# Splitting some steps' exponentials between ScalarE and VectorE, and reordering the last parts, in a two-layer conv-attention kernel

## The chip, the cores and the metric

The kernel runs on one core of a Trainium2 chip. The metric is device time in microseconds (us) of that core. A core has five engines that run their own instruction queues in order: TensorE (PE: matmuls), VectorE (DVE), ScalarE (ACT: exponentials and other functions), GpSimd (POOL) and SyncE (SP, which here issues nearly all DMAs). They wait for each other through semaphores. Matmul results go to PSUM, everything else lives in SBUF or in device memory.

## What is computed

The input is `x`, 4 images of 64x64 pixels with 128 channels, all fp32. The reference, cut to what matters here:

```
# layer 0, per image (N = 4096 pixels)
c2 = conv3x3(conv3x3(elu(x), W1), W2);  a, b = split(c2);  c3 = a * sigmoid(b)
q, k, v = c3 @ Wq, c3 @ Wk, c3 @ Wv                     # 4, 4 and 16 columns
x = x + c3 + (softmax(strictly causal q k^T / 4) @ v, tiled 8 times) @ W3
# layer 1, per image
t = layernorm(x)                                        # 4096 tokens
q, k, v = t @ wq, t @ wk, t @ wv                        # 16 heads of 8
h = t + (softmax(q k^T) @ v) @ wo                       # all 4096 x 4096 pairs, 16 heads
t = x + h + (silu(h @ w1) * (h @ w3)) @ w2              # hidden 344
y = layernorm(t);  out = t + mixture of 8 experts, the best 2 of them by a router
```

By far the most work is in the attention of layer 1: 4 images x 16 heads x 4096 x 4096 exponentials, that is 1.07e9 of them, or 8.4e6 for each of the 128 lanes of an engine.

## The kernel before

All of it is in `fast_path` (line 116). (A second function, `general_path`, is a fallback for inputs with large scores and isn't run with these inputs.) Every engine is used through `InOrder` (line 95), which keeps an engine's instructions in the order in which the Python code emits them. So the order of the emission is the order of each queue.

**The attention step** (`attention_step`, line 772) is the unit of the main loop. A segment is a group `g` of four heads, a chunk `c` of 512 queries and a range of key tiles; a step is one tile of 128 keys `kt` of a segment. There are 4 images x 4 groups x 8 chunks x 32 key tiles = 4096 steps. A step has two halves:

- `scores()` takes two PSUM tiles of 128x1024 from `s_tile` (pool `f_ps_s`, line 134, which holds three such tiles in turn), fills each with two matmuls (`s<-qx,f_kx`, one per head), and lets ScalarE take the exponential of each into an SBUF tile `e` (pool `f_ep`, 8 tiles).
- `values()` multiplies the four heads' exponentials with the values (`acc<-e,vg`, four heads) and adds up in one PSUM bank `acc` over the key tiles of the segment. At the segment's last tile VectorE copies `acc` to `at`, and SP writes it to memory (`d_a<-at`).

**The turn.** The main loop (lines 1190 to 1214) makes one step a turn: `do_step` emits the step's scores and exponentials and puts its `values` on the list `undone`; `finish(2)` at the end of the turn emits the values of the step before the last two. So TensorE works two steps behind ScalarE with the values. The steps of layer 0's attention (`first_step`, 144 of them) go through the same loop when they are there.

**Fillers.** All other work is cut into pieces by Python generators and put between the steps: `first_attention` (line 528, the convolutions, layer 0's attention and the operands of layer 1 of the next image) and `last_part` (line 815, one per chunk: output projection, feed-forward, router, experts). A generator yields after each piece of TensorE work of about 0.46 us; "held" means that the same PSUM bank is filled further, "stop" that an operation of another engine follows. `insert()` (line 239) emits one piece. A turn emits at most one piece, when `credit` is above zero; `credit` grows each turn by a rate such that the fillers (planned at `PREPARE` = 149.0 us an image and `LAST` = 20.8 us a chunk, line 1179) come out spread over the remaining steps, and is capped at 0.7. Pieces use the single PSUM bank `m` (`m_tile`). Some yields carry no TensorE work (0.0): they are turns in which a chain waits for a DMA or another engine. `last_part` has eight of them at its start (its operands are loaded; the reciprocal of the sums goes to memory and comes back broadcast as `per`) and six before the small product with the experts' biases (`eb`), whose operand `g8` goes to memory and back.

After the last step the loop ends, and `run_alone` emits what is left of the fillers: with at least the last chunk's whole `last_part`, since its attention has only just ended.

Of the kernel before, what the change touches and what calls it, by code (L numbers as in the profile page):

```python
# [92 lines left out]


class InOrder:


    def __init__(self, tc, engine):
        self._tc, self._engine, self._last = tc, engine, None

    def __getattr__(self, name):
        op = getattr(self._engine, name)

        def call(*args, **kw):
            made = op(*args, **kw)  # L105
            if self._last is not None:
                after = mybir.DependencyInfo(mybir.DependencyClass.NoSync, mybir.DependencyReason.DATA)
                self._tc.add_manual_dep(made.ins, self._last, after, reason="as written")
            self._last = made.ins.name
            return made  # L110

        return call
# [3 lines left out]
def fast_path(ctx: ExitStack, tc: tile.TileContext, a: dict, where: dict, out: bass.AP, verdict):  # L116
# [12 lines left out]
    big = ctx.enter_context(tc.tile_pool(name="f_big", bufs=1))  # L129
    ep = ctx.enter_context(tc.tile_pool(name="f_ep", bufs=8))  # L130
    wk = ctx.enter_context(tc.tile_pool(name="f_wk", bufs=2))
# [18 lines left out]
    def chunk(tag, name=None):  # L150
        return wk.tile([P, QB], FP, tag=tag, bufs=CHUNKS.get(tag, 1), name=name or tag)

    def small(name, dims):
# [67 lines left out]

    steps_in, undone, fillers = [], [], []

    def do_step(step):
        scores, values = step
        undone.append((values, scores()))

    def finish(leave):
        while len(undone) > leave:
            values, es = undone.pop(0)  # L230
            values(es)

    def advance(part):
# [70 lines left out]
    def spread(eng, taps, u_all):  # L304
# [23 lines left out]
        spread_of.append(u_all)  # L328

    def row_terms(band):  # L330
        r = wk.tile([P, 4, 8, IMG + 2], FP, tag="r", bufs=1, name="r")
        for i, (x, y, op) in enumerate(SUMS):
            pool.tensor_tensor(r[:, i], band[:, x : x + 15 : 2, :], band[:, y : y + 15 : 2, :], op)
        return r
# [267 lines left out]
    def second_operands(b, st):  # L602
# [58 lines left out]
        for k in range(4):  # L661
            product(by_g[:, k], yT[:, k * P : (k + 1) * P], wv1)
            if k == 1:
                yield 0.46, "held"
        vc = wk.tile([P, 4 * NH1, 1 + HD1], FP, tag="vc", bufs=1, name="vc")
        pool.memset(vc[:, :, 0:1], 1.0)
# [30 lines left out]
    def first_step(c, r, qx0, sums, found):  # L697
# [49 lines left out]

        return scores, values

# [21 lines left out]

    def attention_step(b, seg, kt, place, qx, vg, part):
        g, c = seg.g, seg.c

        def scores():
            ss, es = [s_tile(), s_tile()], []
            for j in range(NSLOT):
                r = slice(j * SLOT, (j + 1) * SLOT)
                pe.matmul(
                    ss[j // 2][:, (j % 2) * QB : (j % 2 + 1) * QB],  # L780
                    lhsT=kx[r, place * P : (place + 1) * P].bitcast(FR),
                    rhs=qx[r, :].bitcast(FR),
                    start=True,
                    stop=True,
                )
            for s in ss:
                e = e_tile()
                act.activation(e, s, AF.Exp)
                es.append(e)
            return es  # L790

        def values(es):
            for j in range(NSLOT):
                pe.matmul(
                    acc[j * SLOT : j * SLOT + 1 + HD1, :],
                    lhsT=vg[:, kt // 4, kt % 4, j, :],
                    rhs=es[j // 2][:, (j % 2) * QB : (j % 2 + 1) * QB],
                    start=kt == seg.lo,
                    stop=kt == seg.hi - 1,
                )  # L800
            if kt == seg.hi - 1:
                at = chunk("at1")
                if part:
                    dve.tensor_tensor(at, acc, part[0], ALU.add)
                else:
                    dve.tensor_copy(at, acc)
                to = scratch[b]["a"][c, g] if seg.hi == NT else scratch[b]["p"][g, c]
                sp.dma_start(out=to, in_=at)
                if seg.hi == NT and g == NG1 - 1:
                    fillers.append([last_part(b, c), LAST])  # L810

        return scores, values


    def last_part(b, c):
        d = scratch[b]
# [8 lines left out]
        for _ in range(3):  # L825
            yield 0.0, "stop"
        dve.reciprocal(rs, rs)
# [4 lines left out]
        )  # L832
        for _ in range(4):
            yield 0.0, "stop"
        dve.tensor_tensor(an, an, per, ALU.mult)
        yield 0.0, "stop"
        ps = bank()
# [100 lines left out]
        for b_ in range(4):  # L938
            sp.dma_start(out=g8.rearrange("e (k b a) -> b e k a", k=4, a=SLOT)[b_], in_=by_block[b_, :NE])
        for _ in range(6):  # L940
            yield 0.0, "stop"

        ps = bank()
        tokens(ps, g8, eb, range(2))
        yield 0.46, "held"
        tokens(ps, g8, eb, range(2, 4))
        dve.tensor_tensor(t, ps, t, ALU.add)
        yield 0.46, "stop"
        for k in range(4):
            tk = t[:, k * C : (k + 1) * C]  # L950
            by_e = wk.tile([P, NE, C], FP, tag="two", bufs=1, name="by_e")
            for half in range(2):
# [8 lines left out]
                if half == 1:  # L961
                    added = chunk("w", "added")[:, :C]
                    dve.tensor_reduce(added, by_e.rearrange("p e c -> p c e"), AX.X, ALU.add)
                    dve.tensor_tensor(tk, tk, added, ALU.add)
                yield 0.46, "stop"
        sp.dma_start(out=tb_o[b][:, 4 * c : 4 * c + 4, :], in_=by_k(t))

# [151 lines left out]
    steps_left = [sum(s.hi - s.lo for s in plan if s.b == b) for b in range(B)]  # L1119
    now, quiet = [0], [False]  # L1120

    def stream():
# [16 lines left out]
        for at, seg in enumerate(plan):  # L1139
# [13 lines left out]
            for kt in range(seg.lo, seg.hi):  # L1153
# [3 lines left out]
                if seg.lo > 0 and kt == seg.lo + 4:  # L1157

                    part.append(chunk("part"))
                    sp.dma_start(out=part[0], in_=scratch[seg.b]["p"][seg.g, seg.c])  # L1160
                yield attention_step(seg.b, seg, kt, 8 * seg.place(kt // 8) + kt % 8, qx, vg, part)
                if follower and follower not in ahead and follower.ready():
# [15 lines left out]

    PREPARE, LAST = 149.0, 20.8
    st = batches[0]  # L1180
# [4 lines left out]

    fillers.extend([gen, PREPARE] for gen in reversed(left[1:]) if gen is not st.conv)

    steps = stream()
    credit, waiting = 0.0, False
    while True:  # L1190
        if steps_in:
            do_step(steps_in.pop(0))
        else:
# [4 lines left out]
            if waiting:  # L1198
                finish(0)
            else:  # L1200
                do_step(step)
        b = now[0]
        if batches[b].second == NQ and len(batches) == b + 1 and b + 1 < B:
            Batch(b + 1)
            fillers.append([first_attention(b + 1, batches[b + 1]), PREPARE])

        rate = 1.0
        if batches[b].second == NQ:
            within = steps_left[b] - 40 if b + 1 < B else min(steps_left[b] - 40, 160)
            rate = sum(us for _, us in fillers) / max(1, within)  # L1210
        credit = min(0.7, credit + rate)
        if waiting or credit > 0.0 and not quiet[0]:
            credit -= insert()
        finish(2)
    finish(0)
    alone[0] = True
# [718 lines left out]
```

## Time and profile before

| what | value |
|---|---|
| time of the runs, median of 3 | 8253.63 us (8251.3 to 8255.63) |
| the profiled execution: its time | 8256.29 us |
| the profiled execution: first to last instruction (span) | 8254.1 us |
| mean granted TensorE clock | 0.985 |
| busy: PE | 8010.7 us (97%) |
| busy: ACT | 7886.0 us (96%) |
| busy: DVE | 2513.9 us (30%) |
| busy: POOL | 712.2 us (9%) |
| instructions: DVE / ACT | 5118 / 8699 |
| main loop, roughly | 220 us to 8171 us of the span |

All times below are of the one profiled execution unless it is said otherwise; its own time is 8256.29 us, 2.66 us above the median of the runs. An entry of the timeline gives the start in us from the span's start, the length in us, the engine, the line, the operation, the tiles written and read, and how many equal ones were merged. Since every engine is used through `InOrder`, all instructions carry the line of that helper (L105), so that one goes by the names of tiles. "Busy" of TensorE is the union of the matmuls' intervals; matmuls overlap, so it is no measure of how near to its limit TensorE is. Likewise an exponential's interval (about 1.1 us) is longer than the distance between the ends of two that follow each other.

### The profile page before, as it was taken

How to read it: one execution, taken by the hardware profiler on the slowest of the kernel's cores; microseconds unless marked ns; L12 is line 12 of the kernel's file. 1: busy time of each engine (PE TensorE's matmuls, PEld its weight loads, DVE VectorE, ACT ScalarE, POOL GpSimd, SP SyncE). 2: the span in 40 equal slices, each digit the busy share in tenths (PEclk: the TensorE clock that was granted, in tenths of full speed). 3: DMA queues.
4: the chain of work that ended last, by engine and by line, in shares of the span. 5: the costliest groups of instructions: out<-in, count | busy, mean ns of one | idle time of the engine just before them, and what ended most of it. 6: DMA issues, size and time to landing. Idle time of an engine off the chain costs nothing.

```text
span 8254.1 us, 172356 instructions
## 1 busy us (share of the span) xinstructions
PE 8010.7 (97%) x72957; PEld 2492.4 (30%) x72957; DVE 2513.9 (30%) x5118; ACT 7886.0 (96%) x8699; POOL 712.2 (9%) x631
## 2 busy tenths in 40 slices
PE   4899999999999999999999999999999999999997
PEld 3222222223332322333333333233333333332233
DVE  7433222222322223333322222343332222221223
ACT  1799999999999999999999999999999999999996
POOL 5101211000000003110000000311100000000000
PEclk8899999999999999999999999999999999999998
DMA  1222010101100001111100000111111111111211
GB/s 51 76 69 68 24 41 31 55 29 50 42 24 28 26 19 35 36 39 45 39 31 24 27 28 19 33 36 48 35 42 49 47 38 46 52 37 38 66 61 37
DMA packets 213937, 334.19 MB, mean 40 GB/s; under 512 B 31555, under 2 KB 107811, under 8 KB 213155
## 3 DMA queue, kind: packets, MB, share of 16 engines
q1 hardware_dynamic: 209139, 321.31, 11.9%
q8 instruction: 574, 9.40, 0.5%
q10 hardware_dynamic: 4016, 1.77, 0.1%
q14 instruction: 208, 1.70, 0.1%
HBM read 195.09 MB, written 127.93 MB: 39 GB/s over the span
## 4 chain that ended last, share of the span: by engine, by line
PE 86%; issue 7%; DVE 3%; ACT 1%; DMA 1%; POOL 1%; SPq 0%; ACTq 0%; POOLq 0%; DVEq 0%
PE acc L105 41%; PE s L105 29%; PE m L105 16%; ACT e L105 1%; DVE h L105 1%; POOL v L105 0%; DVE t L105 0%; DMA xe<-in_x_dram 0%; DMA f_kx<-d_k 0%; SPq L105 0%; POOL rs L105 0%; DMA d_r<-sums 0%; DVE added L105 0%; DVE sums L105 0%; POOL xt L105 0%
## 5 line engine op out<-in xcount | busy, mean ns | idle before, releaser
L105 ACT ACTIVATE e<-s 128x1024 f32<-128x1024 f32 (+1 forms) x8480 | 7813.8, 1101 | 100.5 <-PE s L105 95.5
L105 PE MATMUL acc<-e,vg 128*9 128x512 f32 x32768 | 4337.4, 595 | 1.4 <-DVE at L105 1.4
L105 PE MATMUL s<-qx,f_kx 32*128 32x512 f32 (+2 forms) x16960 | 2918.2, 496 | 49.2 <-ACT e L105 33.5
L105 PEld LDWEIGHTS s<-qx,f_kx 32*128 32x128 f32 (+1 forms) x16960 | 1168.8, 182 | 4105.3 <-ACT e L105 3882.9
L105 PEld LDWEIGHTS acc<-e,vg 128*9 128x9 f32 x32768 | 717.0, 90 | 797.2 <-issue 462.1
L105 PE MATMUL m<-v,f_wino 128*32 128x256 f32 x5328 | 432.2, 397 | 5.4 <-DVE t L105 3.5
L105 DVE TENSOR_TENSOR by_e<-m,gates 128x512 f32<-128x512 f32 x245 | 169.5, 692 | 682.0 <-PE m L105 682.0
L105 POOL TENSOR_TENSOR v<-r 128x1024 f32<-128x1024 f32 x128 | 248.7, 1949 | 1172.8 <-PE m L105 1152.4
L105 PE MATMUL m<-f_we,y2T 128*32 128x256 f32 x3920 | 313.1, 391 | 0.0
L105 POOL TENSOR_TENSOR rs<-ve,f_minus_half 128x4 f32<-128x4 f32 x64 | 65.2, 1019 | 2864.4 <-DVE ve L105 2864.4
L105 DVE COPY sd<-m 128x512 f32<-128x512 f32 x166 | 114.8, 692 | 611.3 <-PE m L105 611.3
L105 POOL TENSOR_TENSOR t<-t,h 128x512 f32<-128x512 f32 x32 | 40.8, 1276 | 2530.1 <-DVE h L105 2530.1
L105 DVE TENSOR_REDUCE added<-by_e 128x128 f32<-128x1024 f32 x128 | 255.7, 1998 | 4.4
L105 DVE TENSOR_TENSOR t<-m,t 128x512 f32<-128x512 f32 x62 | 42.9, 692 | 698.5 <-PE m L105 698.5
L105 DVE COPY at<-acc 128x512 f32<-128x512 f32 x130 | 89.9, 692 | 539.9 <-PE acc L105 533.7
L105 PE MATMUL m<-hT,f_fw 128*32 128x256 f32 (+1 forms) x2728 | 236.1, 391 | 0.0
L105 DVE TENSOR_TENSOR t<-m,sums 128x256 f32<-128x256 f32 x126 | 53.5, 425 | 434.3 <-PE m L105 434.3
L105 DVE SCALAR_TENSOR_TENSOR h<-m,h 128x512 f32<-128x512 f32 (+1 forms) x93 | 64.2, 690 | 353.1 <-ACT th L105 255.0
L105 DVE COPY h<-m 128x512 f32<-128x512 f32 (+1 forms) x93 | 64.2, 690 | 314.2 <-PE m L105 314.2
L105 PEld LDWEIGHTS m<-v,f_wino 128*32 128x32 f32 x5328 | 106.5, 109 | 173.9 <-issue 144.0
L105 PE MATMUL m<-e,f_v 128*32 128x512 f32 (+2 forms) x1128 | 150.8, 579 | 0.0
L105 ACT ACTIVATE sd<-s 128x512 f32<-128x512 f32 x26 | 15.5, 597 | 118.8 <-DVE t L105 60.8
(251 smaller groups left out, 3451.5 us busy)
## 6 DMA issues: line engine op xcount, KB each, us to landing
f_kx<-d_k SPq DMA_DIRECT2D x139, 512.0 KB
qx<-d_q SPq DMA_DIRECT2D x152, 256.0 KB
d_q<-two SPq DMA_DIRECT2D x64, 512.0 KB
d_a<-at SPq DMA_DIRECT2D x128, 256.0 KB
vg<-d_v SPq DMA_DIRECT2D x32, 576.0 KB
d_k<-two SPq DMA_DIRECT2D x32, 512.0 KB
d_v<-vc SPq DMA_DIRECT2D x32, 288.0 KB
xe<-in_x_dram SPq DMA_DIRECT2D x32, 256.0 KB
```

Of the source, the lines that this page charges most:

```text
L105: made = op(*args, **kw)
```

## The change

Two things are changed, and the accounting that places them.

**1. Late steps.** In some steps VectorE makes the exponentials of two of the four heads. ScalarE takes the first PSUM tile only (into `ea`). VectorE reads the second tile into an SBUF tile `z`, scaled by log2(e), and then computes 2^z in place in two halves of 512 columns, eight operations each (`powers`): rounding by adding a large constant, the fraction, a polynomial of degree five by Horner's rule, the exponent's bits by a shift, and their product. These 16 operations are not emitted at once: `settle(1.5)` at the end of each turn emits them one by one while an account of VectorE's load, kept in `InOrder` (0.15 us plus 1.06 ns an element, minus the turn's time), is under 1.5 us. When all are emitted and at least three turns have passed, the step's values are emitted (`add_late`) in a turn in which the account of TensorE's lead has room for 0.97 us. Only one late step is under way at a time. At a segment's last tile an unfinished late step is finished at once, whatever it takes (`settle(None)`).

**2. TensorE's lead.** Where before a piece was inserted whenever `credit` was positive, now an account `ahead` of TensorE's lead over ScalarE decides: a turn adds ScalarE's time (0.92 us an exponential), and takes off 0.43 for scores, 0.97 for values and the piece's own time. A step becomes late if `ahead` is above 0.4 and the fillers are not behind (`credit` under 2.6); a piece is inserted if 0.46 us of lead is left and the turn before was not late. The lead is capped at 0.9 us, and at 0.1 us after a late step. `credit` is capped at 3.0 instead of 0.7.

**3. Last parts.** `operands` is split off from `last_part`, so that the next chunk's loads and its reciprocal are started from within the expert loop of the one before (`fetch_following`). The product with the experts' biases is moved behind the expert loop, and the six empty turns before it are gone. `PREPARE` and `LAST` become 143.3 and 18.9.

**4. Room in SBUF.** The pool `f_ep` has 6 tiles instead of 8, and `vc` shares a tile with `two` or `r`.

In the built program, 211 of the 4096 steps are late: 211 fewer exponentials on ScalarE, 211 x 17 = 3587 more operations on VectorE; TensorE's matmuls are the same in number and size.

The core of the diff:

```diff
     def __getattr__(self, name):
         op = getattr(self._engine, name)
         def call(*args, **kw):
             made = op(*args, **kw)
+            sizes = [int(np.prod(ap.shape[1:])) for ap in (*args, *kw.values()) if hasattr(ap, "shape")]
+            self.load += 0.15 + 1.06e-3 * max(sizes, default=0)
...
-    ep = ctx.enter_context(tc.tile_pool(name="f_ep", bufs=8))
+    ep = ctx.enter_context(tc.tile_pool(name="f_ep", bufs=6))
...
     def do_step(step):
-        scores, values = step
-        undone.append((values, scores()))
+        scores, values, late = step
+        es = scores()
+        if late is None:
+            undone.append((values, es))
+        else:
+            slow.append((values, es, late, turn[0]))
...
+    def settle(limit):
+        if slow:
+            todo = slow[0][2]
+            while todo and (limit is None or dve.load < limit):
+                todo.pop(0)()
+    def settled():
+        return bool(slow) and not slow[0][2] and turn[0] > slow[0][3] + 2
+    def add_late():
+        values, es, _, _ = slow.pop(0)
+        values(es)
+    def powers(z):
+        todo = []
+        for h in range(2):
+            zh = z[:, h * QB : (h + 1) * QB]
+            t, q = late_tile("t"), chunk("part", "q")
+            todo.append(lambda t=t, zh=zh: dve.tensor_scalar(t, zh, MAGIC, None, ALU.add))
+            todo.append(
+                lambda t=t, zh=zh: dve.scalar_tensor_tensor(zh, t, MAGIC, zh, ALU.subtract, ALU.subtract)
+            )
+            todo.append(lambda q=q, zh=zh: dve.scalar_tensor_tensor(q, zh, POLY[4], zh, ALU.add, ALU.mult))
+            for k in (3, 2, 1):
+                todo.append(
+                    lambda q=q, zh=zh, k=k: dve.scalar_tensor_tensor(q, q, POLY[k], zh, ALU.add, ALU.mult)
+                )
+            bits = t.bitcast(mybir.dt.int32)
+            todo.append(lambda bits=bits: dve.tensor_scalar(bits, bits, 23, None, ALU.logical_shift_left))
+            todo.append(
+                lambda t=t, q=q, zh=zh: dve.scalar_tensor_tensor(zh, q, POLY[0], t, ALU.add, ALU.mult)
+            )
+        return todo
...
     def attention_step(b, seg, kt, place, qx, vg, part, late):
         def scores():
...
+            if late is not None:
+                e, z = late_tile("ea", 1024), late_tile("z", 1024)
+                act.activation(e, ss[0], AF.Exp)
+                dve.tensor_scalar(z, ss[1], LOG2E, SHIFT, ALU.mult, ALU.add)
+                late.extend(powers(z))
+                return [e, z]
...
         def values(es):
+            if kt == seg.hi - 1 and slow:
+                settle(None)
+                add_late()
...
     def last_part(b, c):
...
+        while fetch(b, c):
+            yield 0.0, "stop"
+        t, h, an = fetched.pop((b, c))
...
-        for _ in range(6):
-            yield 0.0, "stop"
-        ps = bank()
-        tokens(ps, g8, eb, range(2))
-        yield 0.46, "held"
-        tokens(ps, g8, eb, range(2, 4))
-        dve.tensor_tensor(t, ps, t, ALU.add)
-        yield 0.46, "stop"
         for k in range(4):
...
+                fetch_following(b, c)
                 yield 0.46, "stop"
+        ps = bank()
+        tokens(ps, g8, eb, range(2))
+        yield 0.46, "held"
+        tokens(ps, g8, eb, range(2, 4))
+        dve.tensor_tensor(t, ps, t, ALU.add)
+        yield 0.46, "stop"
         sp.dma_start(out=tb_o[b][:, 4 * c : 4 * c + 4, :], in_=by_k(t))
...
+                late = [] if may_be_late[0] and seg.lo == 0 and 2 <= kt <= seg.hi - 8 else None
...
     while True:
+        turn[0] += 1
+        may_be_late[0] = not slow and ahead > 0.4 and credit < 2.6 and not steps_in
+        begun = len(slow)
...
+        late = len(slow) > begun
+        takes = EXP if late else 2 * EXP
+        dve.load = max(0.0, dve.load - takes)
...
-        credit = min(0.7, credit + rate)
-        if waiting or credit > 0.0 and not quiet[0]:
-            credit -= insert()
+        credit = min(3.0, credit + rate)
+        left = ahead + takes - SCORES
+        if len(undone) > 2:
+            left -= VALUES
+        if settled() and left >= VALUES:
+            add_late()
+            left -= VALUES
+        elif waiting or credit > 0.0 and not quiet[0] and (credit > 2.8 or left >= PIECE and not just_late):
+            took = insert()
+            credit -= took
+            left -= took
+        elif late and undone:
+            finish(len(undone) - 1)
+            left -= VALUES
         finish(2)
+        settle(1.5)
+        ahead = min(max(left, 0.0), 0.1 if late else AHEAD)
+        just_late = late
```

## The prediction

> **What bounds the kernel now.** I read the page's busy shares first, then the groups of ScalarE within the main loop (500 to 8170 us), then the timeline of single turns, last the timeline after the last step.
>
> ```profile
> PE 8010.7 (97%) x72957; PEld 2492.4 (30%) x72957; DVE 2513.9 (30%) x5118; ACT 7886.0 (96%) x8699; POOL 712.2 (9%) x631
> ```
> ```profile
> L105 ACT ACTIVATE e<-s 128x1024 f32<-128x1024 f32 x8173 | 7551.2, 1104 | 37.7 <-PE s L105 33.9 <-ACT e L105 1.3 <-PE m L105 0.2
> ```
>
> Both engines look full; only one is. In the loop ScalarE idles 37.7 us before 8173 exponentials: it is the bound. TensorE's busy time is padded by overlapping matmuls. Start to start of the scores, a turn without a piece takes it 1.41 us, with a piece of 0.45 us 1.86. Taking such undisturbed lengths for all turns that the trace shows gives 7044 us of work in 7896 us. VectorE is idle 70%. So moving exponentials to VectorE attacks the right engine; the question is whether TensorE can follow. That is read from single turns: TensorE, then ScalarE:
>
> ```profile
> 2311.05 1.04 PE L105 MATMUL s<-qx,f_kx 32*128 32x512 f32 x4
> 2312.02 1.04 PE L105 MATMUL acc<-e,vg 128*9 128x512 f32 x8
> 2312.99 0.92 PE L105 MATMUL s<-qx,f_kx 32*128 32x512 f32 x4
> 2313.85 1.05 PE L105 MATMUL acc<-e,vg 128*9 128x512 f32 x8
> 2314.82 0.93 PE L105 MATMUL s<-qx,f_kx 32*128 32x512 f32 x4
> ```
> ```profile
> 2310.48 5.63 ACT L105 ACTIVATE e<-s 128x1024 f32<-128x1024 f32 x6
> ```
>
> The first of these six exponentials is 1.05 us long and ends at 2311.53, the sixth at 2316.11: ends lie 0.916 us apart (median over the trace 0.917). Scores take 0.43 us when their four matmuls start together; here they are split: the second pair of the first row starts at 2311.59, 0.06 after that end. With three PSUM tiles, a step's second tile is the one that ScalarE read three tiles ago, so TensorE stands until it is free. Values (0.97) come behind. **The lead is therefore capped.** Scores started at 2312.99 could have their exponential ended 1.62 us later, at 2314.61 (1.62: the turn below, scores at 2452.92, exponential ended 2454.54); it is due at 2315.20. The lead is 0.58 us, not the 0.9 at which the change caps its account. One turn of before tests this:
>
> ```profile
> 2450.49 0.93 PE L105 MATMUL s<-qx,f_kx 32*128 32x512 f32 x4
> 2451.35 0.66 PE L105 MATMUL m<-f_consts,y 128*128 128x128 f32 x4
> 2451.94 1.05 PE L105 MATMUL acc<-e,vg 128*9 128x512 f32 x8
> 2452.92 0.51 PE L105 MATMUL s<-qx,f_kx 32*128 32x512 f32 x4
> ```
>
> Its piece takes 0.59 us, all of the lead; the next exponential ends at 2454.54, 0.92 after the one before: no stall, nothing to spare. More extra work in one turn would stall ScalarE.
>
> [...] the two halves of a step are different tiles, and in this trace exponentials keep 0.917 us beside VectorE's copies from `m`. So the read of `z` should not slow ScalarE. [...] the trace has 692 (`an`). [...] the trace has `neg<-xe` at 422 ns median. [...] during the split above nothing overtakes.
>
> **The change, part by part** (211 late steps, counted in the built program).
>
> *ScalarE, removed:* 211 x 0.917 = 193.5 us on the bounding engine. This is the most that can be had.
>
> *The turn after a late step.* Put the end of its one exponential at 0. The next scores' second tile is that same tile: second pair at 0.05, done 0.485, values to 1.46, the following scores' exponential can end at 1.46 + 1.63 = 3.09. ScalarE has only two exponentials between and wants it at 3 x 0.917 = 2.75: stall 0.34. So a late step cannot gain more than the lead. In the built order 169 late steps are followed by values without a piece, and 14 have values in their own turn and none in the next, which comes out the same (183 x 0.34 = 62); 28 have values and a piece in the next turn (0.34 + 0.445 each, 22). Sum 84 us. (Most late turns carry a piece and no values; that piece is free, and the values come later.)
>
> *The turn of the late values.* All 211 stand in a turn with the ordinary values: 0.97 more work against a lead of 0.57: stall 0.40, 84 us.
>
> *The turns behind both* begin with no lead; each that carries a piece (1.865 against 1.834) costs 0.031, until the first turn without one. Counting in the built order at most four such turns each (before, too, four use up the lead of 0.13 that a piece leaves): 409 behind late steps, 333 behind late values, 742 x 0.031 = 23 us.
>
> So the late steps give 193.5 - 84 - 84 - 23 = 2 us: they pay back what they take. The cover is the lead of 0.57.
>
> *VectorE's load.* A late step adds one read of 1024 (1.22, the row `top<-two`), 4 one-source operations (0.42) and 12 two-source ones (0.69): 11.2 us, 2.36 ms in all; VectorE comes to 59%. The queue is in order: behind them stand copies that free `m`, for which the next piece waits, and the late values wait for the last of the 16. In 109 of 211 cases the kernel's account of VectorE's load is at 1.5 us or more just before the late values, which come 0.43 us into the next turn. Bounds: nothing, or 109 x 1 us; the negative is excluded, since no operation of VectorE is taken away. I take 0.25 us each, 27 us, pieces included.
>
> *Unfinished late steps.* At six segment ends 1 to 7 operations are still to be emitted, 25 in all: 25 x 0.66 - 6 x 0.57 = 13 us on the path (from 5, if they ran ahead, to 17).
>
> *Last parts.* In the loop their empty turns lie beside ScalarE: nothing, now and after; if the cover went, the loads (some 9 us from `sums<-d_a` to `per`) would show. Behind the loop the chain counts:
>
> ```profile
> 8173.24 0.33 SPq L105 DMA_DIRECT2D d_a<-at  x1
> ...
> 8180.43 0.59 SPq L105 DMA_DIRECT2D sums<-d_a  x1
> ...
> 8221.88 0.31 DVE L105 STREAM_TRANSPOSE turned<-gates 128x128 f32<-128x128 f32 x1
> ...
> 8228.09 2.04 PE L105 MATMUL s<-f_eb,g 8*128 8x128 f32 x8 [11.07 <-DMA g<-d_g]
> ...
> 8232.17 0.69 DVE L105 TENSOR_TENSOR by_e<-s,gates 128x512 f32<-128x512 f32 x1 [1.31 <-PE s L105]
> ...
> 8246.70 0.29 DVE L105 TENSOR_TENSOR t<-t,added 128x128 f32<-128x128 f32 x1
> ```
>
> Here `sums` waits on SP behind the output of the chunk before; in the new order that chunk is finished in the loop, and only `d_a`'s landing is waited for (3 us, as `d_r` from 8183.14 to 8186.16, plus a little for its size): 8176.6, 3.8 saved. The experts can start at 8222.2 instead of 8232.17: four times 3.45 us (8240.04 to 8243.48) ends at 8236.0, plus 0.7 for the biases, against 8247.0: 10.2 saved. Sum -14 us (between -8 and -16). SP's queue has only this chunk left then. In the loop the loads pulled ahead go through SP before later keys and queries, which are fetched a segment ahead: nothing, or some us if a `d_r` holds SP.
>
> *SBUF.* Six `e` tiles hold three steps; the values two steps back are always emitted before the scores that follow: nothing. The `vc` in `r` follows GpSimd's reads, which GpSimd has done by then: nothing, up to 5 us if not. The startup's order is unchanged.
>
> **Sum.** -2 + 27 + 13 - 14 = +24 us on the profiled 8256.3: 8280. That execution lies 2.7 above the median of the runs; so 8278. A measurement of this kernel can tell about 0.2% (16 us) from no change.
>
> **Rivals.** (1) *Faster:* ScalarE's saving is real and the late values hide. It decides at the lead in the turn of the late values: from 0.97 on, their stall and the penalty behind them (84 + 10) vanish: 8278 - 94 = 8184; without the stall after late steps too, 8278 - 191 = 8087. For it: ScalarE is the bound with 37.7 us of idle time, and TensorE has 850 us to spare. Against: the split scores, which cap the lead wherever ScalarE bounds. (2) *VectorE becomes the wait.* If at the 109 late values 1 us is waited for, and the pieces as well, 27 becomes 95: 8346. For: an in-order queue at 59%, near full in the 8 to 10 turns behind a late step, and 12 two-source operations that GpSimd may slow (`pos<-xe,neg` averages 782 ns against 692). Against: the account limits what is queued. (3) *It cancels:* as forecast, but VectorE hides: 8251 to 8264.
>
> **Chances.** Forecast (mostly 8240 to 8320) 0.60, rival 1 0.25, rival 2 0.10, rival 3 0.05. Rival 1 lies below 8237. Of the forecast's weight about 0.40 lies above 8270, 0.18 down to 8237 and 0.02 below. So faster 0.27, same 0.23, slower 0.50. The range leaves out the deepest of rival 1 and the worst of rival 2: 8160 to 8335.
>
> **What would show it.** Right: exponentials' ends 1.26 us apart (0.917 + 0.34) two tiles after a late step; a gap of about 0.4 us more in the turn of the late values; 211 fewer exponentials, but as long a loop; the tail from the last values to the end 14 us shorter. Wrong: scores not split in the turn after a late step, or ends 0.917 apart through the late values (rival 1); TensorE waiting for `z` or for VectorE's copies by more than 60 us in the list of waits (rival 2).

## The result, and the profile after

The changed kernel takes 8444.79 us (median of 4 runs, 8443.48 to 8451.53), the kernel before 8254.44 (4 runs beside them). The ratio is 1.0233, with a 95% interval of 1.022 to 1.0246: it is 2.3% slower, +190 us. The prediction was +24 us. It had the side right and the size wrong: 8444.79 lies above the whole range (8160 to 8335), and above the 8346 of the rival that came nearest, "VectorE becomes the wait". The profiled execution took 8444.1 us, its span 8442.2.

The busy shares of the kernel after, and the first row of its costliest groups; "idle before" at the end of a row is the time in which the engine stood ahead of them, with what ended it:

```profile
PE 8002.3 (95%) x72993; PEld 2470.2 (29%) x72993; DVE 4854.7 (58%) x8705; ACT 7766.0 (92%) x8488; POOL 754.1 (9%) x631
...
L116 ACT ACTIVATE e<-s 128x1024 f32<-128x1024 f32 (+1 forms) x8058 | 7515.1, 1057 | 404.2 <-PE s L116 391.2
```

The same row of before, over its whole span:

```profile
L105 ACT ACTIVATE e<-s 128x1024 f32<-128x1024 f32 (+1 forms) x8480 | 7813.8, 1101 | 100.5 <-PE s L105 95.5
```

VectorE's share is the one that was forecast (59%, now 58). ScalarE has 120 us less to do, yet it stands for 391.2 us before its exponentials, waiting for TensorE's scores, where before it stood for 95.5. Reckoned from one exponential's end to the next, the time above 0.917 us summed over all of them went from 123 to 502 us, +379. The 211 exponentials removed are worth -193.5, ScalarE's 244 other instructions among them, with the waits ahead of these, take 19 us longer (188.5 before, 207.1 after), and the work behind the last exponential is 15 us shorter: +379 - 193.5 + 19 - 15 = +189, for the 188 us by which the span grew.

The waits of TensorE in the loop (500 to 8160 us; total, times, longest, all in us but the times), the longest five of the kernel after and the longest one of before:

```profile
PE s L116 <- ACT ea L116: 60.7, 179, 0.8
PE s L116 <- ACT e L116: 51.3, 86, 4.9
PE acc L116 <- DVE z L116: 44.5, 32, 7.2
PE m L116 <- DVE by_e L116: 25.2, 30, 1.9
PE m L116 <- DVE sd L116: 22.6, 20, 2.4
```
```profile
PE s L105 <- ACT e L105: 30.1, 51, 4.1
```

Of the five, before has only the second. The first is the forecast stall behind late steps: the scores' second tile is still ScalarE's. The other three are VectorE: late values that wait for `z`, pieces that wait until `m` has been copied. Together 92 us on TensorE alone, where the prediction named 60 as the mark of rival 2.

First the forecast stall. TensorE's and ScalarE's timelines around a late step (its `ea` starts at 3037.19):

```profile
3037.47 0.50 PE L116 MATMUL s<-qx,f_kx 32*128 32x512 f32 x2
3038.30 0.50 PE L116 MATMUL s<-qx,f_kx 32*128 32x512 f32 x2 [0.34 <-ACT ea L116]
3038.73 1.04 PE L116 MATMUL acc<-e,vg 128*9 128x512 f32 x8
3039.71 0.51 PE L116 MATMUL s<-qx,f_kx 32*128 32x512 f32 x4
```
```profile
3037.19 1.05 ACT L116 ACTIVATE ea<-s 128x1024 f32<-128x1024 f32 x1
3038.10 1.99 ACT L116 ACTIVATE e<-s 128x1024 f32<-128x1024 f32 x2
3040.31 2.89 ACT L116 ACTIVATE e<-s 128x1024 f32<-128x1024 f32 x3 [0.23 <-PE s L116]
```

The scores of the next turn split at 3038.30, right behind `ea`'s end at 3038.24; the values follow, then the scores at 3039.71, and the exponential that needs them ends 0.33 us late. That is the "ends 1.26 us apart" of the prediction. Summed over the third exponential behind each late one it is 83 us (84 were forecast).

Then what was not forecast. VectorE, GpSimd, TensorE and ScalarE at the longest stall of the loop, one timeline each:

```profile
3081.28 6.33 DVE L116 SCALAR_TENSOR_TENSOR q<-q,z 128x512 f32<-128x512 f32 x3
3087.53 2.14 DVE L116 TENSOR_SCALAR t<-t 128x512 int32<-128x512 int32 x1
3089.70 2.29 DVE L116 SCALAR_TENSOR_TENSOR z<-q,t 128x512 f32<-128x512 f32 x1
```
```profile
3082.51 8.94 POOL L116 TENSOR_TENSOR v<-r 128x1024 f32<-128x1024 f32 x4
```
```profile
3092.05 1.02 PE L116 MATMUL acc<-z,vg 128*9 128x512 f32 x1 [7.24 <-DVE z L116]
...
3096.29 1.84 PE L116 MATMUL acc<-e,vg 128*9 128x512 f32 x8
```
```profile
3096.46 1.94 ACT L116 ACTIVATE e<-s 128x1024 f32<-128x1024 f32 x2 [10.41 <-PE s L116]
```

While GpSimd makes four `v` (and an `r` before them), five operations of the polynomial take 10.8 us instead of 3.2 (four of 0.69, one of 0.42). The late values stand ready in TensorE's order ahead of everything else and wait 7.24 us for `z`; ScalarE is idle for 10.41. Afterwards TensorE is slow as well: the values at 3096.29 take 1.84 us instead of 1.04.

Last, the chain behind the loop: the rows of the timeline of after that answer to those shown of before:

```profile
8376.70 0.33 SPq L116 DMA_DIRECT2D d_a<-at  x1
8378.72 0.57 SPq L116 DMA_DIRECT2D sums<-d_a  x1
...
8419.84 0.31 DVE L116 STREAM_TRANSPOSE turned<-gates 128x128 f32<-128x128 f32 x1
```

`sums` is issued 2.0 us behind `d_a` (before 7.2), and the experts begin right behind `turned`. From `d_a` to the end of the span it is 65.5 us (8442.2 - 8376.70); before it was 80.9.

### The profile page after: what moved, and what is told of

The parts are those of the page before. It is cut to its first block, busy times and chain, and to the rows that moved or that the text cites. A ratio compares the mean times of both kernels' runs of the same rounds, so it can differ in the third digit from the quotient of the medians.

```text
span 8442.2 us, 175372 instructions
## 1 busy us (share of the span) xinstructions
PE 8002.3 (95%) x72993; PEld 2470.2 (29%) x72993; DVE 4854.7 (58%) x8705; ACT 7766.0 (92%) x8488; POOL 754.1 (9%) x631
## 5 line engine op out<-in xcount | busy, mean ns | idle before, releaser
L116 ACT ACTIVATE e<-s 128x1024 f32<-128x1024 f32 (+1 forms) x8058 | 7515.1, 1057 | 404.2 <-PE s L116 391.2
L116 PE MATMUL acc<-e,vg 128*9 128x512 f32 x31080 | 4198.8, 597 | 1.8 <-DVE at L116 1.8
L116 PE MATMUL s<-qx,f_kx 32*128 32x512 f32 (+1 forms) x16960 | 2802.7, 497 | 138.3 <-ACT ea L116 62.3
L116 DVE SCALAR_TENSOR_TENSOR q<-q,z 128x512 f32<-128x512 f32 x1266 | 924.1, 730 | 34.9
L116 DVE TENSOR_SCALAR z<-s 128x1024 f32<-128x1024 f32 x211 | 258.1, 1223 | 308.3 <-PE s L116 298.7
L116 POOL TENSOR_TENSOR v<-r 128x1024 f32<-128x1024 f32 x128 | 252.1, 1975 | 1280.6 <-PE m L116 1259.2
L116 PE MATMUL acc<-z,vg 128*9 128x512 f32 x844 | 298.8, 601 | 46.4 <-DVE z L116 45.3
L116 DVE SCALAR_TENSOR_TENSOR z<-q,t 128x512 f32<-128x512 f32 x422 | 312.6, 741 | 10.8
L116 DVE SCALAR_TENSOR_TENSOR q<-z 128x512 f32<-128x512 f32 x422 | 311.5, 738 | 12.5
L116 DVE SCALAR_TENSOR_TENSOR z<-t,z 128x512 f32<-128x512 f32 x422 | 307.8, 729 | 12.6
L116 ACT ACTIVATE ea<-s 128x1024 f32<-128x1024 f32 x211 | 227.2, 1077 | 3.9 <-PE s L116 3.8
```

## The experiments

The theory behind the first runs: the lead of TensorE takes back what the late steps give, as forecast; the loss comes from the polynomials in VectorE's queue. All times are medians. Each kernel was timed beside the kernel before, which took 8252.8 to 8254.8.

### No late step, and the last parts alone

```diff
-        may_be_late[0] = not slow and ahead > 0.4 and credit < 2.6 and not steps_in
+        may_be_late[0] = False
```

> The changed kernel, but no step is made late: every exponential is ScalarE's again; the new account that places pieces, the six e tiles and the new order of the last parts stay. Theory: the late steps cause the whole loss, and the last parts give their 14 us behind the loop: 8240 us (8230 to 8255). Rival: the new placing of pieces (held back up to a credit of 2.8, fewer e tiles, loads fetched one part ahead) costs the time itself: then most of the loss stays, 8350 us or more.

Measured: 8231.3 us, ratio 0.9972 (0.9962 to 0.9983). The rival falls: without late steps nothing of the loss is left, whatever the new placing costs. 8231 is the base from here on. The second kernel also takes pieces by the old rule:

```diff
-        credit = min(3.0, credit + rate)
+        credit = min(0.7, credit + rate)
...
-        elif waiting or credit > 0.0 and not quiet[0] and (credit > 2.8 or left >= PIECE and not just_late):
+        elif waiting or credit > 0.0 and not quiet[0]:
```

> No late step, and pieces are placed by the rule of the kernel before (credit capped at 0.7, taken whenever it is positive): what is left of the change is the new order of the last parts, the smaller costs that the planner gives them, and six e tiles. Theory: only the 14 us behind the loop are saved, 8240 us, the same as with the new account within 10 us. Rival: the account of TensorE's lead places pieces better or worse than the old rule: then the two runs without late steps lie over 20 us apart.

Measured: 8219.6 us, ratio 0.9959 (0.9945 to 0.9973). This is the fastest kernel of the study, below both. The theory missed by 20 us, on the good side; the two placings lie 12 us apart, so the new one is the dearer by that much. Of the 33 us won, 15 are behind the loop. The others are in the loop, where ScalarE's stalls sum to 102 us against 123 before. One kind that has gone is seen in the timeline of before, the kernel without polynomials:

```profile
3453.38 4.83 DVE L105 TENSOR_SCALAR h<-xt,mv,rs 128x128 f32<-128x128 f32 x4 [1.13 <-POOL rs L105]
3453.40 4.73 POOL L105 TENSOR_TENSOR r<-f_c_band 128x528 f32<-128x528 f32 x4
...
3458.26 0.47 PE L105 MATMUL m<-f_consts,h 128*128 128x128 f32 x1 [0.94 <-DVE h L105]
```

Here a layernorm's four `h` meet GpSimd's `r`; each takes about 1.2 us, the transposes wait for them, and ScalarE stood 3.10 us before 3461.39. With the last parts in their new order `h` takes 462 ns on average instead of 688, and the wait for `h` (9.3 us, 12 times) is gone from the list. That this makes up all of the 18 us was not tried by itself.

### The late steps without their polynomials

```diff
-        todo = []
-        for h in range(2):
...
+        def skip():
+            dve.load += 0.15 + 1.06e-3 * QB
+
+        todo = [skip] * 16
```

> The changed kernel with the same order of turns, but the 16 operations of each polynomial are left out, so that a late step's second half is only read out of PSUM (heads of the late steps get wrong weights); their estimates are still added to the account of VectorE's load, so the placing stays as it is. VectorE then has as much to do as before plus 211 reads. Theory: waits for VectorE (late values waiting for z, pieces waiting for copies that stand behind a polynomial, and the slow turns of TensorE after the long ones) cost 150 to 190 us, the capped lead the rest: 8285 us (8255 to 8320). Rival A: the lead alone costs the time, and VectorE hides: 8430 us or more. Rival B: the lead does not cap anything and VectorE alone costs the time: 8240 minus 194, about 8050 us.

Measured: 8231.0 us, ratio 0.9974 (0.9965 to 0.9983): the base, to 0.3 us. So 211 exponentials fewer, with VectorE out of the way, gain **nothing**. ScalarE's stalls rose from 108 (no late step) to 290 us, +182, against the 193.5 removed: 82 in the third exponential behind a late one, 65 in the turns of the late values, 35 elsewhere. In TensorE's list of waits the row of `ea` is as in the changed kernel, and those of VectorE have all but gone (`by_e` 4.2 us, `sd` 1.5):

```profile
PE s L116 <- ACT ea L116: 62.0, 183, 0.8
```

The theory's 8285 missed, since it put 150 to 190 us on the polynomials; they cost **213.8 us** (8444.8 - 8231.0). Rival A, VectorE hidden, and rival B, no cap on the lead, both fall.

### Whose tile is first

```diff
-                act.activation(e, ss[0], AF.Exp)
-                dve.tensor_scalar(z, ss[1], LOG2E, SHIFT, ALU.mult, ALU.add)
+                dve.tensor_scalar(z, ss[0], LOG2E, SHIFT, ALU.mult, ALU.add)
+                act.activation(e, ss[1], AF.Exp)
                 late.extend(powers(z))
-                return [e, z]
+                return [z, e]
```

> The changed kernel, but VectorE takes the first PSUM tile of a late step and ScalarE the second. The scores that follow need the tile of the late step that was written second; in this order it is still ScalarE's, but their first tile is free earlier and the tile that the following scores split on is VectorE's, read 1.2 us after it was written and not at the end of a second exponential. Theory: the wait of 0.34 us behind late steps goes in most of the 177 places where it is seen: 73 us less, 8370 us (8350 to 8420, the upper end if VectorE's read of z stands in its queue). Rival: it doesn't matter which tile is whose: 8445 us within 10.

> The two edits of the runs before together: VectorE takes the first PSUM tile of a late step, and the polynomials are left out (heads of late steps get wrong weights). Each alone gave 8437 and 8231 us. Theory: the swap does take away the wait of 0.34 us behind late steps, and gained only 7 us because the read of z then stood in VectorE's full queue; with that queue empty it shows: 8231 - 73 = 8158 us (8145 to 8190). Rival: the swap moves the wait to another place whatever VectorE does: 8231 us within 10.

Measured: 8437.5 us with polynomials (ratio 1.0222, 1.0205 to 1.0239) and 8226.5 without (0.9965, 0.9951 to 0.9979). The theory fell both times: 7 and 5 us instead of 73. The trace of the second shows why. Two late steps, TensorE's timeline, the first with the wait and the second without:

```profile
3033.59 0.50 PE L116 MATMUL s<-qx,f_kx 32*128 32x512 f32 x2
3034.44 0.50 PE L116 MATMUL s<-qx,f_kx 32*128 32x512 f32 x2 [0.34 <-ACT ea L116]
```
```profile
4490.30 0.90 PE L116 MATMUL s<-qx,f_kx 32*128 32x512 f32 x4
```

The pool doesn't hand the three tiles out in a fixed circle. In the built program of the change the second pair of the scores behind a late step has ScalarE's tile to wait for in all 211 cases. With the swap it has VectorE's in 126, but in the other 85 the tile comes one pair later, the second pair still gets ScalarE's, and nothing is won. The trace agrees: in the median the third exponential is 0.06 us late in the 126 cases and 0.33 in the 85. Its sum went only from 82 to 73 us, because in some of the 126 VectorE's read of `z` came late and the scores waited for that instead. TensorE's waits ahead of scores, over the whole span, without the swap (first two rows) and with it:

```profile
PE s L116 <- ACT ea L116: 62.6, 185, 0.8
PE s L116 <- DVE z L116: 1.4, 4, 0.4
```
```profile
PE s L116 <- ACT ea L116: 28.6, 82, 0.4
PE s L116 <- DVE z L116: 26.9, 61, 1.2
```

The swap moves the wait; it doesn't take it away.

### The late values, the ends and the queue

First only the earliest turn of the late values (`last_op` is the turn of the last polynomial operation); then, in the last line, with late steps farther from a segment's end as well:

```diff
-        return bool(slow) and not slow[0][2] and turn[0] > slow[0][3] + 2
+        return bool(slow) and not slow[0][2] and turn[0] > last_op[0] + 2
...
                 todo.pop(0)()
+                last_op[0] = turn[0]
...
-                late = [] if may_be_late[0] and seg.lo == 0 and 2 <= kt <= seg.hi - 8 else None
+                late = [] if may_be_late[0] and seg.lo == 0 and 2 <= kt <= seg.hi - 12 else None
```

> The changed kernel, and late values come at the earliest three turns behind the last polynomial operation; late steps may stand as near to a segment's end as in the change (206 late steps, 25 of them cut short by an end, 8 with operations left, 31 in all). With late steps 12 tiles away from the end as well, the time was 8318 us. Theory: the early values were the larger part, the ends cost about 0.66 us for each operation left: 8318 + 20 = 8340 us (8322 to 8365). Rival: the distance from the ends did it, and holding alone wins little: 8395 us or more.

> The changed kernel, but the values of a late step come at the earliest three turns behind its last polynomial operation (before: the next turn), and late steps keep 12 tiles away from a segment's end, so that they are done by then: 187 late steps. VectorE's queue stays as full as it was. Theory: of the 213 us that the polynomials cost, 131 us are the late values that wait for z (68 us) and the longer stall in their turn (63 us more than without polynomials); these go, and 187/211 of the other 82 stay: 8231 + 73 = 8304 us (8280 to 8340). Rival: the loss lies in the pieces that wait for copies behind the polynomials, and holding the values helps little: 8231 + 187 x 1.01 = 8420 us (over 8380).

Measured: 8345.6 us for the values alone (206 late steps, ratio 1.0115, 1.0098 to 1.0132), 8318.5 for both (187, ratio 1.0076, 1.0059 to 1.0093). Both as the theory had them. Holding the values wins 99 us, the ends 27.

The queue, with late steps 16 tiles from an end as well (`seg.hi - 16` in the last line above):

```diff
-        settle(1.5)
+        settle(0.7)
```

> The changed kernel, but an operation of a polynomial is put into VectorE's queue only while the account of its load is below 0.7 us (before 1.5), so two of them a turn at most, and late steps keep 16 tiles away from a segment's end: 129 late steps. Theory: with a queue that empties every turn neither copies nor z are waited for much: 8231 + 129 x 0.2 = 8257 us (8235 to 8290). Rival: what is queued doesn't matter, each late step costs what it cost (213 us by 211 steps, 1.01 us): 8361 us (over 8330).

Measured: 8265.3 us (129 late steps, ratio 1.0013, 1.0007 to 1.002), as the theory had it: 34 us above the base, 0.26 us a late step instead of 1.01. Part of this gain belongs to the ends, which were not separated here.

Short queue, held values (one turn less), distant ends and the swap together:

> All three: VectorE takes the first PSUM tile, at most two polynomial operations a turn, late values at the earliest two turns behind the last of them, late steps 16 tiles away from a segment's end: 123 late steps. Theory: the wait of 0.34 us goes as well (42 us), and nothing of VectorE is waited for: 8231 - 42 + 10 = 8199 us (8180 to 8230), below both kernels and below the last parts alone (8220). Rival: VectorE's read of z still comes late, and the swap gives nothing: 8245 to 8290 us.

Measured: 8247.7 us (123 late steps, ratio 0.999, 0.9984 to 0.9997). Missed: it is 16 us above the base, within the rival's range (8245 to 8290). With what the swap's own runs showed this is no surprise.

### GpSimd beside the polynomials

```diff
-        may_be_late[0] = not slow and ahead > 0.4 and credit < 2.6 and not steps_in
+        may_be_late[0] = not slow and ahead > 0.4 and credit < 2.6 and not steps_in and bool(fillers) and fillers[0][2] is not None
```

> The changed kernel with one condition more: a step is made late only while the part being inserted is a last part, in which GpSimd does next to nothing: 123 late steps. VectorE's queue, the late values and the segment ends stay as they are. Turn by turn, against the same plan without polynomials, the 55 late steps with a two-source operation slowed beside GpSimd lost 121 us (2.2 each), the 156 others 99 us (0.635 each). Theory: GpSimd's share goes, the rest stays: 8231 + 123 x 0.635 = 8309 us (8290 to 8325). Rival: GpSimd has no part in it, each late step costs the mean: 8231 + 123 x 1.04 = 8359 us (over 8340).

Measured: 8292.0 us, ratio 1.0048 (1.0031 to 1.0064): 0.49 us a late step over the base instead of 1.01. The theory holds, by somewhat more than it claimed. The edit also takes late steps away from all pieces of `first_attention`, so these pieces themselves are a rival to GpSimd. The changed kernel's trace, set turn by turn against that of the same plan without polynomials, decides it. Where no two-source operation of a late step was slowed (none above 0.9 us, which leaves 53 slowed steps and not the 55 of the expectation), the step lost 0.65 us beside `first_attention` (48 steps) and 0.62 beside last parts (110); where one was, 2.44 (44 steps) and 1.48 (9). So it is the slowed operations that cost, not the kind of piece. What remains is VectorE's own queue: TensorE still waits for `by_e` (21.6 us, 33 times) and for `z` (12.2 us, 7 times).

Then all of it at once, with the tiles as in the change: no GpSimd, `settle(0.7)`, values two turns behind the last operation, 16 tiles from an end.

> The changed kernel with four conditions: late steps only while a last part is inserted (no GpSimd beside them), at most two polynomial operations a turn, late values two turns behind the last of them, 16 tiles away from a segment's end: 76 late steps, whole polynomials, the tiles as in the change. Theory: the four take away all that the polynomials cost, and a late step gives back what it takes, as without polynomials: 8231 + 76 x 0.05 = 8235 us (8222 to 8248). Rival: the polynomials cost something else as well, at least 0.3 us each: 8254 us or more.

Measured: 8234.8 us, ratio 0.9978 (0.997 to 0.9985), 3.6 us above the base with 76 whole polynomials, 0.05 us each. In TensorE's list of waits those for VectorE are back to nothing, and that for `ea` stays:

```profile
PE s L116 <- ACT ea L116: 22.3, 66, 0.8
...
PE m L116 <- DVE by_e L116: 2.5, 6, 0.6
```

So under these four conditions together the polynomials cost next to nothing (the same 76 steps without polynomials were not timed); and a late step whose polynomial is free still gains nothing.

### Late values in two halves

```diff
-        values, es, _, _ = slow.pop(0)
-        values(es)
+        values, es, _, _ = slow[0]
+        if half[0] == 0 and not both:
+            half[0] = 2
+            values(es, range(2))
+        else:
+            slow.pop(0)
+            heads, half[0] = range(half[0], NSLOT), 0
+            values(es, heads)
...
-            left -= VALUES
+            left -= VALUES / 2
```

> The changed kernel without polynomials (heads of late steps get wrong weights) as before, and the values of a late step are added in two halves of two heads each, in two different turns, each 0.485 us instead of 0.97: 248 late steps, since each is over sooner. Theory: TensorE's lead is 0.57 us, so a half fits into it and the stall in the turn of the late values (65 us over 211 steps without polynomials) goes; what stays per late step is 0.39 us in the turns behind it and about 0.16 elsewhere: 8231 - 248 x (0.92 - 0.55) = 8140 us (8125 to 8185). Rival: the lead isn't what the late values miss; splitting them changes nothing: 8231 us within 15.

> All three edits that gave 8248 us together, with polynomials, and late values added in two halves in two turns: 133 late steps. Theory: the 41 us of stall in the turns of late values go: 8205 us (8190 to 8225), below the last parts alone (8220). Rival: 8248 us within 10, late steps then cannot pay.

> All edits: VectorE takes the first PSUM tile, at most two polynomial operations a turn, late values two turns behind the last of them and in two halves, 16 tiles away from a segment's end, and only while a last part is inserted: 81 late steps. Theory: each late step gains 0.92 and pays 0.35 behind it and 0.1 elsewhere: 8231 - 81 x 0.45 = 8195 us (8180 to 8215). Rival: a late step gains nothing even so: 8225 us or more.

Measured: 8297.9 us without polynomials (ratio 1.0052, 1.0035 to 1.0068), 8302.4 with all edits (1.006, 1.0043 to 1.0077), 8268.8 with all edits and only beside last parts (1.0017, 1.001 to 1.0023). All three missed, by 158, 97 and 74 us, the first two on the bad side of their rivals too. The timeline of the first shows a turn with half of the late values between two starts of scores:

```profile
3765.58 0.50 PE L116 MATMUL s<-qx,f_kx 32*128 32x512 f32 x4
3766.01 0.60 PE L116 MATMUL acc<-ea,vg 128*9 128x512 f32 x2
...
3766.47 1.43 PE L116 MATMUL acc<-e,vg 128*9 128x512 f32 x6
3767.84 0.52 PE L116 MATMUL s<-qx,f_kx 32*128 32x512 f32 x4
```

Start to start it is 2.26 us; without late values a turn takes 1.41. Half the values cost 0.85 us, hardly less than the whole (0.97). The eight matmuls of four heads, of about 0.60 us each, overlap: four start within 0.02 us of each other, four more 0.43 us later, and all are over in 1.04 us. The four of two heads also take two starts, two of them at 3766.01 and two at 3766.45, 0.44 us apart. The edit meant to halve the suspected cost so nearly doubled it. As an experiment that serves as well: with 1.7 us instead of 0.97 for most late steps (210 of 248; in the others both halves fell into one turn) the stalls in the turns of late values rose from 65 us (211 turns) to about 160 (458 turns), and the time by 67 us. The late values do run into the end of the lead, by about a third of a us each time.

## Why the prediction was right and wrong

- *What bounds the kernel, and the lead.* Right, and the strongest part: the lead is 0.57 us, too little for late values of 0.97, so that late steps pay back what they take. Its comparison with the account's 0.9 was too mild, though. The account counts that at a turn's end and then adds the next turn's spare 0.44 (1.84 - 0.43 - 0.97), so it lets 1.34 us of extra work into one turn where 0.57 fits. No run lowered that cap (`AHEAD`). Forecast +2 us gained without VectorE; measured 0.2 (8231.3 without late steps, 8231.0 with them and no polynomials).
- *The turn after a late step.* 84 us forecast, 82 to 83 measured, 0.33 us each for 0.34.
- *The turn of the late values.* 84 us forecast, 65 measured without polynomials: 0.31 us each for 0.40.
- *The turns behind both.* 23 us forecast. The stalls without polynomials leave 182 - 82 - 65 = 35 for these and all other places; they were not told apart.
- **VectorE's load: the step that failed.** The prediction took "0.25 us each, 27 us, pieces included", with bounds of "nothing, or 109 x 1 us". Together with the next term, 40 us; measured 213.8. The mechanism was named, even as rival 2, but its size was wrong in three ways. First, the count: only the 109 late values with a full account were charged; the pieces, said to be included, got no charge of their own, but those whose copies stand behind a polynomial wait as well. Second, the duration: 0.69 us was taken for operations of which `q<-q,z` takes 1.52 us on average beside GpSimd (below). Third, the range: a late value that is not ready holds up all that follows it in TensorE's order, so one wait can be 7.24 us, and the bound of 1 us was no bound. Turn by turn, against the same plan without polynomials, the 55 late steps with slowed operations lost 121 us and the 156 others 99. By edits, holding the values wins 99 us. The two overlap: the longest wait for `z` is one beside GpSimd. Of the 221 us between the two profiled spans (8442.2 and 8221.3) about half stands in TensorE's list: in the loop its waits for VectorE rise from 21.7 to 128.5 us. How the rest divides stays open; at most some 32 us of it (an estimate: half of the 65 us by which the time at half the clock grew in the loop, 72 to 137) is TensorE's lower clock (0.50, below).
- *Unfinished late steps.* 13 us forecast; moving late steps away from the ends won 27, with 19 late steps fewer. Right in kind, but its size was not measured: with the values held, 25 late steps were cut short by an end, 8 of them with operations left, so the case is another one.
- *Last parts.* -14 us forecast behind the loop, 15 measured: `sums` issued 5.2 us sooner, the biases no longer ahead of the experts. "In the loop ... nothing" was wrong by 18 us in the good direction with the old placing, 6 with the new one. Part of that is a layernorm that no longer meets GpSimd; the rest stays open.
- *SBUF.* Nothing forecast. It was not tried alone; the six `e` tiles are in every kernel here, the fastest too.
- *The rivals.* Rival 1 needed the stall of the late values to vanish; no edit made it. Rival 2 was the right one, and its 8346 was 99 us too low. Its term of 95 us is even less than the 109 x 1 us that it names, before any piece is counted. The chances gave it 0.10; a queue that is in order and near full, with operations that GpSimd may slow, deserved more.

Without VectorE's term the sum would have been right: 8278 - 40 = 8238 forecast, 8231 measured.

## What to carry to other kernels

Work taken off the bounding engine gains only as much as the next engine can run ahead; read that lead from start to start in the timeline (here 0.57 us, and of 193.5 us taken off 0.2 were gained; the split scores point to the three PSUM tiles, whose number was not varied), and an account that assumes more places work where it stalls. Before filling an idle in-order engine, ask what stands behind the new work in its queue and who waits for that, and take its durations from moments when its neighbours are busy too (here `q<-q,z`: 0.69 us alone, 1.52 beside GpSimd). The part of a change that shortens a chain can be worth keeping when the rest is not: the last parts alone gave 8220 us, 0.4% below the kernel before.

## What the runs showed of the hardware

**VectorE beside GpSimd.** In the changed kernel `q<-q,z` takes 690 ns on average where GpSimd is idle throughout (1199 times) and 1523 where it is busy for more than 0.4 of it (61 times); the shift `t<-t`, with one source, 418 and 1285. GpSimd suffers less: its `v<-r` takes 1975 ns on average, 1949 before, its `r<-f_c_band` 1392, 1256 before. So beside GpSimd the operation with two sources took 2.2 times as long on average, the one with one source 3.1 times. Why they are slowed was not shown. The prediction had seen 782 against 692 in an average and not split it.

**TensorE's clock after a wait.** The granted clock in the kernel after: before and after a wait of 1.81 us that ended at 3827.64, after another of 1.81 us that ended at 3255.41, and after the one of 7.24 us. The columns are us, PE busy (instructions), clock, DMA share, GB/s:

```profile
3824.00:3827.60 3.60, 1.83 (x20) 1.00 0.00 0
3827.60:3831.50 3.90, 3.86 (x28) 0.60 0.02 4
...
3255.40:3259.40 4.00, 4.00 (x36) 1.00 0.00 0
...
3092.00:3097.00 5.00, 4.95 (x18) 0.50 0.00 0
```

Around some of TensorE's waits its granted clock is 0.50 instead of 1.00, in stretches of 3.4 to 10.2 us, so that these waits cost more than their own length: the values at 3828.10 take 1.65 us instead of 1.04. Not every wait does this. Of the 25 in the loop of 1.5 to 3 us that began at the full clock, 10 came with such a stretch, and of the 8 longer ones all; it began during the wait or at most 1.1 us behind its end. Of the two waits of 1.81 us above, the first was followed by the lower clock and the second was not; what decides it was not shown. It is a small part of the whole: groups of values at the low clock cost 26 us in the kernel after and 13 before.

**Half the heads, nearly the same time.** Values of two heads took 0.85 us, from one start of scores to the next (2.26 with them, 1.41 without), and of four 0.97.
